# A two-layer graph attention kernel: the turn of the layers with three accumulators and chunk-wise reuse of tiles, and the prologue's weight folds on TensorE

## The chip, the cores and the metric

The kernel runs on one core of one Trainium2 chip. The metric is the device time of one launch in microseconds (us); the number given for a version is the median of its runs. A profile is of one further execution, which has a time of its own.

## The reference

6250 nodes with 256 features each, 200,000 edges sorted by their destination, two graph attention layers (4 heads of 64, then 1 head of 256), and a residual around both. Cut to what matters:

```python
def _add_self_loops(src, dst, ea, n):
    cnt = segment_sum(ones, dst, n);  sm = segment_sum(ea, dst, n)
    loop = sm / maximum(cnt, 1.0)[:, None]
    return concat([src, arange(n)]), concat([dst, arange(n)]), concat([ea, loop])

def _gat(x, src, dst, ea, Wg, a_s, a_d, Wge, a_e, b, n, h, f):
    hx = (x @ Wg).reshape(n, h, f)
    he = (ea @ Wge).reshape(-1, h, f)
    al = leaky_relu(einsum('nhf,hf->nh', hx, a_s)[src] + einsum('nhf,hf->nh', hx, a_d)[dst]
                    + einsum('ehf,hf->eh', he, a_e), 0.2)
    al = exp(al - segment_max(al, dst, n)[dst])
    al = al / segment_sum(al, dst, n)[dst]
    return segment_sum(hx[src] * al[:, :, None], dst, n).reshape(n, h * f) + b

h0 = maximum(layernorm(x), 0)
te = relu(edge_attr @ We0 + be0) * exp(h0 @ Wo0 + bo0)[src][:, None]
h1 = relu(_gat(h0, *_add_self_loops(src, dst, te, n), Wg0, as0, ad0, Wge0, ae0, bg0, 4 heads) + h0)
te = relu(edge_attr @ We1 + be1) * exp(h1 @ Wo1 + bo1)[src][:, None]
h2 = _gat(h1, *_add_self_loops(src, dst, te, n), Wg1, as1, ad1, Wge1, ae1, bg1, 1 head) + h1
return x + h2 + h0
```

All arithmetic is float32.

## The kernel before

**Tables and gathers.** For each layer a table in DRAM holds one row per node: the features times `Wg`, the node's two attention terms, and its edge factor `exp(x @ Wo + bo)`. Layer 0's table (`T[0]`, 268 numbers a row) is written in the prologue, layer 1's (`T[1]`, 260 numbers) step by step as layer 0's nodes are finished. The edges of a layer are cut into 66 steps: 64 of 24 chunks with 128 edges each, and two shorter ones at the end, 132 steps in all, numbered through both layers (step 66 is layer 1's first). For every chunk POOL issues one indirect DMA (L905) that gathers the rows of the chunk's 128 source nodes into one chunk (270 words a partition) of a tile `G`. Step k's `G` comes from the pool `gp[k % 3]`; step 0 uses a tile of its own, `G0`, whose rows are computed in the prologue instead of gathered from the table. POOL works in order: a gather that waits holds all gathers behind it.

**A step.** With the rows there, a step computes edge logits, segment maxima by scans, weights `kw`, scaled rows, and then `sums` (L1285): for each chunk two matmuls with a one-hot matrix `S` that `onehots` (L1095, 3.3 us of DVE) makes from the destination numbers. The sums of a step are merged into its nodes, and, one step later, `rows1`, `rows2` and `rows3` finish them; in layer 0 the finished row (`t1row`, one of two buffers in turn) is stored by SP into `T[1]` (L1419) and into a node table `nd` (L1421, L1424).

**The prologue.** 49 tiles of 128 nodes in nine groups of 2, 5, 7, 7, 7, 7, 7, 5 and 2 are loaded from `x` (L225, SP), and each passes through statistics (`stats`: `BN_STATS` and `BN_AGGR` on DVE, then a chain of small operations for the inverse root, on POOL for the groups from the fourth on), `norm` (ACT, L319), `turn` (PE transposes, L325, and an ACT copy, L327), `mult` (PE, L439) and `keep` (DVE, L443); a group's rows are stored into `T[0]` by SP (L344). Behind them come 24 tiles of gathered `x` rows (L255), in groups of 6 and 18, which end in `G0`. The loop over `k` (tiles) fixes the order on every engine: in each turn `step` issues the next operation of some group's statistics, and small pieces of other work (`index`, the edges' index tables; `rows0`, the gathers of `x` rows) are put in between. Before the tiles, `fold` and `fold_e` multiply the attention vectors into the weights: `Wg` times `as` and `ad` summed over a head's features give extra columns of the weight tile. They do so on DVE (L181, L183, L192, L194), from rows that a broadcast DMA spreads over all partitions; layer 1's folds run later, in the first steps (`soon`, `late`). POOL clears four node tiles `tw` (L264). `idle` gives PE nine large matmuls ahead of the first tile.

**The turn of the layers** (`ending`; a, b, c are steps 63, 64, 65, and `after` is step 66). Step 66 gathers from `T[1]` before the last rows of it are stored: its `gather` goes early into step a's tile `G`, chunk by chunk. The rows that were still lacking are read again later (`lack_rows`, L1073) and put in place by `complete` (L1083, L1084): for each of the 24 chunks two matmuls of the lacking rows with two one-hot matrices, and one DVE operation that adds the result to the kept rows. The one-hots are made by `select` (L1066, two operations of DVE) from a list of source rows, `row`. The list and the second one-hot lie in a tile of the pool `gp[2]`, the pool that step 68's gathers take their tile from next; the first one-hot lies in a tile of the one-hots' own pool. `complete` is a generator that `ending` draws from in three parts, between `parts`, `blocks`, `edge_rows` and the others of step 66. PE writes chunk c of it into accumulator c mod 3: two halves of one PSUM tile `y`, and a tile `fin`.

Of the kernel before, what the change touches and what calls it, by code (L numbers as in the profile page):

```python
# [22 lines left out]
F32 = mybir.dt.float32  # L23
# [8 lines left out]
P = 128  # L32
# [47 lines left out]
class Kernel:  # L80
# [32 lines left out]
    def consts(self, wp):  # L113
# [4 lines left out]
        self.wg, row, wpk = [], [], []  # L118
        pool = (wp, cp)
        self.ones = cp.tile([P, 1], F32, name="ones")  # L120
        nc.gpsimd.memset(self.ones, 1.0)
        self.bias, self.webd, self.be, wge = [], [], [], []
        def weights(L):

            q = (nc.scalar, nc.sync)[L.l]
            wg = cp.tile([P, 2, L.MW], F32, name=f"wg{L.l}")
            q.dma_start(wg, a[f"wg{L.l}"].rearrange("(k p) m -> p k m", p=P))
            r = pool[L.l].tile([P, 3, D], F32, name=f"row{L.l}", bufs=1)
            q.dma_start(r.rearrange("p k d -> p (k d)"), a[f"row{L.l}"][0:3 * D].partition_broadcast(P))
# [3 lines left out]
            row.append(r)  # L133
            b = cp.tile([P, L.MW], F32, name=f"bias{L.l}")
            nc.sync.dma_start(b, a[f"row{L.l}"][3 * D:].partition_broadcast(P))
            w = cp.tile([P, P + 1], F32, name=f"webd{L.l}")
            nc.sync.dma_start(w, a[f"we{L.l}"][:, 0:P + 1])
            e = pool[L.l].tile([P, D], F32, name=f"wge{L.l}", bufs=1)
            nc.sync.dma_start(e, a[f"we{L.l}"][:, P + 1:])
# [3 lines left out]
            wge.append(e)  # L143
# [31 lines left out]
        def fold(L):  # L175

            H = L.H
            for k in range(2):
                for j, c0 in ((0, L.p), (1, L.ad)):
                    t = pool[L.l].tile([P, D], F32, name=f"wtmp{L.l}", bufs=2)  # L180
                    V.tensor_mul(t, self.wg[L.l][:, k, 0:D], row[L.l][:, j, :])  # L181
                    yield
                    V.tensor_reduce(self.wg[L.l][:, k, c0:c0 + H], t.rearrange("p (h f) -> p h f", h=H),  # L183
                                    axis=AX.X, op=OP.add)
                    yield

        def fold_e(L):

            H = L.H
            wea, we1 = self.wea[L.l]  # L190
            t = pool[L.l].tile([P, D], F32, name=f"wtmp{L.l}", bufs=2)
            V.tensor_mul(t, wge[L.l], row[L.l][:, 2, :])  # L192
            yield
            V.tensor_reduce(we1, t.rearrange("p (h f) -> p h f", h=H), axis=AX.X, op=OP.add)  # L194
            yield
# [5 lines left out]
        self.late, self.soon = fold_e(self.L[1]), fold(self.L[1])  # L201
# [1444 lines left out]
```

## Time and profile before

| | us |
|---|---|
| runs | 4047.03, 4033.51, 4033.07 |
| median | 4033.51 |
| the profiled execution, its time | 4041.07 |
| its span (first to last instruction) | 4039.3 |
| POOL busy | 2998.3 (74%) |
| PE busy | 2658.8 (66%) |
| DVE busy | 2454.5 (61%) |
| ACT busy | 1117.3 (28%) |
| the first gather from a table starts at | 88.43 |
| the last one starts at | 4010.02 |

A row of the timeline reads: start, duration, engine, line, operation, the tile written and the tiles read, the count, and in brackets how long the engine was idle before and what ended that. In a row of a group the total, the mean of one in ns, and the idle time before them stand behind the count. A row of the windows holds the window, its length, and the busy time and count for PE, PE's weight load, DVE, ACT and POOL, then the granted clock, the DMA share and GB/s. Line numbers are those of the code above; in the changed kernel the same code stands some 15 to 40 lines further down.

### The profile page before, as it was taken

To read this page: it belongs to the slowest core of one execution; us is meant where nothing else is said; L and a number is where in the kernel's file an instruction comes from. 1 tells how busy PE (TensorE), PEld (TensorE's weight loads), DVE (VectorE), ACT (ScalarE), POOL (GpSimd) and SP (SyncE) were. 2 spreads that over 40 slices of the span, in tenths; PEclk is the share of its full clock that TensorE was granted. 3 is DMA by queue.
4 is the path that set the end of the run, shared out by engine and by line. 5 is a ranking of instruction groups with operands and counts; after the bars stand their busy time and mean duration, and the time that the engine had idled before them with its cause. 6 is when DMAs were issued, how large, how long until landed. Compare 5 with 4: busy or idle time off the path is not lost.

```text
span 4039.3 us, 37506 instructions
## 1 busy us (share of the span) xinstructions
PE 2658.8 (66%) x9974; PEld 1744.1 (43%) x9974; DVE 2454.5 (61%) x6096; ACT 1117.3 (28%) x2670; POOL 2998.3 (74%) x3253
## 2 busy tenths in 40 slices
PE   8776676776666676666667656656566566566565
PEld 6444444444444444444444434434334334334343
DVE  7897877877877877877864333344343343343445
ACT  5211111111111111111115434334344344343341
POOL 5777777777777777777757777777777777777775
PEclk9888888888888888888887777777777777777777
DMA  7455555555555555555545455445445445445443
GB/s 245 134 159 145 148 155 147 146 157 143 148 157 146 149 154 144 151 155 142 152 128 151 132 141 142 134 140 140 136 138 143 133 138 144 132 138 143 133 138 97
DMA packets 239747, 585.27 MB, mean 145 GB/s; under 512 B 64315, under 2 KB 96737, under 8 KB 239307
## 3 DMA queue, kind: packets, MB, share of 16 engines
q0 software_dynamic: 150144, 422.75, 39.2%
q1 hardware_dynamic: 88973, 159.40, 12.5%
q8 instruction: 85, 1.39, 0.1%
q14 instruction: 129, 1.06, 0.1%
q10 hardware_dynamic: 416, 0.67, 0.1%
HBM read 544.82 MB, written 38.12 MB: 144 GB/s over the span
## 4 chain that ended last, share of the span: by engine, by line
POOL 32%; DVE 26%; issue 14%; PE 10%; ACT 10%; DMA 8%; DVEq 0%; SPq 0%; ACTq 0%; POOLq 0%
POOL G L905 32%; ACT G L1275 8%; DVE G L1266 7%; DMA G<-T,src 7%; PE y L1005 4%; DVE S L1095 3%; PE u L1285 3%; DVE lb L1029 2%; PE ps L439 1%; DVE m L1214 1%; DVE rt L1144 1%; ACT R L1006 1%; DVE al L1162 1%; DVE al L1160 1%; DVE fb L1175 1%
## 5 line engine op out<-in xcount | busy, mean ns | idle before, releaser
L905 POOL DMA_INDIRECT G<-T,src x3102 | 2946.4, 950 | 989.9 <-issue 912.4
L1285 PE MATMUL u<-G,S 128*128 128x270 f32 (+1 forms) x6252 | 1582.8, 416 | 202.3 <-DVE G L1256 199.0
L1285 PEld LDWEIGHTS u<-G,S 128*128 128x128 f32 x6252 | 1287.4, 207 | 497.0 <-DVE G L1256 225.5
L1275 ACT ACTIVATE G<-G,kw 128x256 f32<-128x256 f32 x1512 | 609.0, 496 | 0.0
L1006 ACT ACTIVATE R<-y,webd 128x1024 f32<-128x1024 f32 (+2 forms) x264 | 235.3, 891 | 1292.9 <-PE y L1005 829.8
L1182 PE MATMUL lf<-ident,fb 128*36 128x128 f32 (+1 forms) x132 | 49.8, 377 | 765.6 <-DVE fb L1175 763.7
L1158 DVE TENSOR_TENSOR G<-rt,G 128x96 f32<-128x96 f32 (+1 forms) x132 | 30.3, 230 | 816.2 <-DMA G<-T,src 815.7
L1266 DVE TENSOR_TENSOR G<-G,kps 128x6144 f32<-128x6144 f32 (+3 forms) x77 | 440.9, 5735 | 0.0
L1095 DVE TENSOR_TENSOR S<-kps,loc 128x3072 f32<-128x3072 f32 x132 | 437.6, 3315 | 4.6
L1005 PE MATMUL y<-ea,webd 64*128 64x256 f32 (+1 forms) x1056 | 386.6, 826 | 49.9 <-ACT R L1006 49.9
L1014 PE MATMUL zad<-R,wea 128*64 128x384 f32 (+1 forms) x1056 | 295.2, 699 | 158.2 <-ACT R L1006 158.2
L1182 PEld LDWEIGHTS lf<-ident,fb 128*36 128x36 f32 (+1 forms) x132 | 15.7, 119 | 806.8 <-DVE fb L1175 804.3
L1014 PEld LDWEIGHTS zad<-R,wea 128*64 128x64 f32 x1056 | 85.2, 182 | 414.3 <-ACT R L1006 334.7
L1290 ACT ACTIVATE U<-u 128x270 f32<-128x270 f32 (+1 forms) x132 | 51.8, 392 | 642.4 <-PE u L1285 642.4
L1317 DVE SCALAR_TENSOR_TENSOR mg<-U,mw 128x1 f32<-128x1 f32 x66 | 14.5, 220 | 281.3 <-ACT mw L1315 281.3
L1005 PEld LDWEIGHTS y<-ea,webd 64*128 64x128 f32 x1056 | 122.7, 284 | 122.7 <-ACT R L1006 68.4
L1248 DVE SCALAR_TENSOR_TENSOR G<-U,kw,G 1x257 f32<-1x257 f32 x62 | 29.6, 478 | 182.6 <-ACT G L1275 182.6
L1116 PE MATMUL zad<-a,Q 128*128 128x12 bf16 (+1 forms) x132 | 26.0, 197 | 157.9 <-DVE a L1111 157.5
L439 PE MATMUL fin<-wg,h1T 128*128 128x260 f32 x264 | 126.5, 629 | 4.3 <-ACT h1T L1380 4.3
L1144 DVE STREAM_TRANSPOSE rt<-zad 128x768 f32<-128x768 f32 (+1 forms) x130 | 126.1, 970 | 4.5 <-PE zad L1130 4.5
L1029 DVE TENSOR_TENSOR lb<-lb,kps 128x1536 bf16<-128x1536 bf16 (+1 forms) x68 | 112.9, 1661 | 0.0
L1390 ACT ACTIVATE t1row<-t1row 128x1 f32<-128x1 f32 x66 | 13.4, 203 | 354.0 <-DVE t1row L443 354.0
(213 smaller groups left out, 2312.1 us busy)
## 6 DMA issues: line engine op xcount, KB each, us to landing
G<-T,src POOLq DMA_INDIRECT x3102, 2.8
ea<-in_ea_dram SPq DMA_DIRECT2D x64, 768.0 KB
lb<-locrow SPq DMA_DIRECT2D x64, 384.0 KB
nd<-t1row SPq DMA_DIRECT2D x66, 225.8 KB
tw<-nd SPq DMA_DIRECT2D x66, 225.8 KB
tw<-T SPq DMA_DIRECT2D x66, 117.2 KB
T<-t1row SPq DMA_DIRECT2D x66, 113.8 KB
tw<-in_x_dram SPq DMA_DIRECT2D x66, 112.0 KB
```

Of the source, the lines that this page charges most:

```text
L439: self.nc.tensor.matmul(ps[:, :L.MW], hT[:, k, :], self.wg[L.l][:, k, :], start=(k == 0), stop=(k == 1))
L905: nc.gpsimd.indirect_dma_start(out=G[:, c, 0:L.TW], out_offset=None, in_=self.T[L.l][0:self.N, :], in_offset=bass.IndirectOffsetOnAxis(ap= ...
L1005: nc.tensor.matmul(y[:, i, :n], self.webd[l][r, :], ea[r, w], start=True, stop=True)
L1006: nc.scalar.activation(R[:, :, w], y[:, :, :n], AF.Relu, bias=self.be[l])
L1014: nc.tensor.matmul(st["zad"][i * PH:(i + 1) * PH, o], self.wea[l][0], R[:, i, w], start=True, stop=False)
L1029: V.tensor_tensor(lb[:, :, :n], lb[:, :, :n], self.k_part.unsqueeze(2).to_broadcast([P, i, n]), op=OP.is_equal)
L1095: nc.vector.tensor_tensor(st["S"][:, c0:c1, :], self.k_iota.unsqueeze(1).to_broadcast(w), self.loc[:, o + c0:o + c1].unsqueeze(2).to_broad ...
L1144: V.transpose(rv[:, :32 * c].rearrange("p (b n) -> p b n", b=2), z.rearrange("p (b n) -> p b n", b=2)[:, :, :16 * c])
L1182: self.nc.tensor.transpose(self.lf[0:e.shape[1], 1:P + 1], e, self.ident)
L1266: nc.vector.tensor_tensor(v, v, pw[:, c0:c1, :].unsqueeze(3) .to_broadcast([P, c1 - c0, H, L.F]), op=OP.mult)
L1275: self.nc.scalar.activation(v, v, AF.Copy, scale=st["w"][:, c:c + 1])
L1285: nc.tensor.matmul(st["u"][:, :L.W], S[:, i, :], G[:, i, 0:L.W], start=(j == 0), stop=(j == c - 1))
```

## The change

In the turn of the layers: `t1row` has three buffers in place of two. `select` makes one one-hot at a call: the first is made ahead of `rows3(c)`, the second at the old place. `complete` accumulates in three tiles (`y`, `fin` and `u`, which is the tile of the sums), its first eight chunks stand ahead of `parts`, and step 66's `onehots` leave this stretch for the ordinary place in the loop. Three tiles are reused chunk by chunk, each gather waiting for what its own chunk held, where a new tile of the pool waited for the whole: `G0` for step 3, the tile of list and second one-hot for step 68, and step 66's own `G` for step 69.

In the prologue: the attention vectors come as a block matrix `att`, and `fold` and `fold_e` are done by PE (two transposes of each 128 rows of the weights, an ACT copy, two small matmuls) at the start and at tiles 12, 24 and 30, for both layers. Six `x` buffers are loaded ahead in place of four. `idle` gives three matmuls in place of nine. The node tiles are cleared by two DMAs in place of POOL's memset. The index work starts later (tile 17 in place of 11). The statistics of the first six gathered rows run between the node tiles from tile 16 on, with their chain on POOL; those of the other 18 from tile 49 on. The first edge loads (`lb`, `ea`, `fl`) are issued behind the prologue's last store.

```diff
-            self.gather(after, a["G"])
+            after["own"] = self.steps[after["k"] + 3]["own"] = a["G"]
+            self.gather(after)
...
         self.rows2(c)
+        if early:
+            self.select(after, 0)
         self.rows3(c)
...
                 self.lack_rows(after)
-                self.select(after)
+                self.select(after, 1)
                 fill = self.complete(after)
...
             self.spread(after)
+            for _ in range(C // 3):
+                next(fill, None)
             self.parts(after)
             self.blocks(after)
-            for _ in range(C // 3):
-                next(fill, None)
...
             self.edge_rows(after)
-            self.onehots(after)
             drain(fill)
+            if not early:
+                self.onehots(after)
...
+        if len(steps) > 3 and steps[3]["L"].l == 0:
+            steps[3]["own"] = self.G0
...
-        X = self.gp[2].tile([P, C, 270], F32, name="G").rearrange("p c d -> p (c d)")
+        G = self.steps[st["k"] + 2]["own"] = self.gp[2].tile([P, C, 270], F32, name="G")
+        X = G.rearrange("p c d -> p (c d)")
...
-        y = self.ps_y.tile([P, 2, 512], F32, name="y")
-        ps = (y[:, 0, :], y[:, 1, :], self.ps_f.tile([P, 512], F32, name="fin"))
+        ps = (self.ps_y.tile([P, 2, 512], F32, name="y")[:, 0, :], self.ps_f.tile([P, 512], F32, name="fin"),
+              self.ps_1.tile([P, 512], F32, name="u"))
...
-        st["trow"] = trow = self.trow1[st["s"] % 2]
+        st["trow"] = trow = self.trow1[st["s"] % 3]
...
+        def sides(w, pt):
+
+            pT = pt.tile([P, 2, P], F32, name="pT")
+            for j in range(2):
+                nc.tensor.transpose(pT[:, j, :], w[:, j * P:(j + 1) * P], self.ident)
+            t = wp.tile([P, 2, P], F32, name="hT", bufs=3)
+            nc.scalar.activation(t, pT, AF.Copy)
+            return t
+
+        def fold(L, pt):
+
+            H, at, wg = L.H, atts[L.l], self.wg[L.l]
+            ps = pt.tile([P, 512], F32, name="ps", bufs=5)
+            ts = [sides(wg[:, i, 0:D], pt) for i in range(2)]
+            for i, t in enumerate(ts):
+                for j in range(2):
+                    nc.tensor.matmul(ps[:, 2 * H * i:2 * H * i + 2 * H], t[:, j, :], at[:, j, 0:2 * H],
+                                     start=(j == 0), stop=(j == 1))
+            yield
...
-            idle(9)
+            idle(3)
+            folds = [fold(L, pt)]
+            next(folds[0])
...
-            for t in self.tws:
-                nc.gpsimd.memset(t, 0.0)
...
-                e = nc.gpsimd if 3 <= g < g0 else V
+                e = nc.gpsimd if 3 <= g <= g0 else V
...
-                    if q > (g if k >= NT - 4 else min(g, g0)):
-                        return
+                    if q > g if q < g0 else k < (16 if q == g0 else NT):
+                        continue
...
-                if k > 10 and k % 2 or k > NT:
+                if k > 16 and k % 2 or k > NT:
                     next(index, None)
...
+                if k == 8:
+                    none = a["x"][N:N + 2 * P, :].rearrange("n d -> (n d)")
+                    for i, e in ((0, 1), (M + 1, P)):
+                        w = self.tw4[i:e].rearrange("p i w -> p (i w)")
+                        n, m = w.shape
+                        nc.sync.dma_start(w, none[0:n * m].rearrange("(p w) -> p w", w=m))
+                if k in (12, 24, 30):
+                    folds.append(fold(self.L[1], pt) if k == 24 else fold_e(self.L[k // 30], pt))
+                    next(folds[0])
+                if k in (14, 26, 32):
+                    drain(folds.pop())
...
-                    self.load_lb(0)
-                    self.load_ea(0)
-                    self.load_fl(0)
...
                     store(kept)
                     kept += 1
+                    if kept == g0:
+                        self.load_lb(0)
+                        self.load_ea(0)
+                        self.load_fl(0)
```

How this moves instructions is shown at three places.

DVE at the turn of the layers, from the last node row of step 65 on, before. `t1row1` is the finished row of step 65, `S_12310` and the second half of `G_12308` are the two one-hots, `G_11781` is step 66's tile:

```order
L1370 TENSOR_TENSOR t1row1_175<-tw4_176,hw_12384 128x256
L1372 TENSOR_TENSOR t1row1_175<-t1row1_175,fb_12395 128x256
L443 TENSOR_TENSOR t1row1_175<-fin_12408,bias1_374 128x260
L1066 TENSOR_TENSOR S_12310<-G_12308,kps_116 128x3072
L1066 TENSOR_TENSOR G_12308<-G_12308,kps_116 128x3072
L1029 TENSOR_TENSOR lb_11982<-lb_11982,kps_116 128x1536
L1030 TENSOR_TENSOR Q_12426<-kps_116,qsel_570 128x256
L1108 CAST a3_12429<-tw4_176 128x1
L1109 TENSOR_TENSOR a3r_12430<-tw4_176,a3_12429 128x1
L1110 CAST a3_12429<-a3r_12430 128x1
L1111 TENSOR_TENSOR a3_12429<-a3r_12430,a3_12429 128x1
L1123 TENSOR_TENSOR aq0_170<-zad_12435,quad_122 128x4x3
```

The same place after; `G_11799` is step 66's tile, and L1121 is the operation that puts a corrected chunk in place (L1084 before):

```order
L1407 TENSOR_TENSOR t1row2_191<-tw4_192,hw_12402 128x256
L1409 TENSOR_TENSOR t1row2_191<-t1row2_191,fb_12413 128x256
L1102 TENSOR_TENSOR S_12328<-G_12326,kps_112 128x3072
L474 TENSOR_TENSOR t1row2_191<-fin_12426,bias1_370 128x260
L1102 TENSOR_TENSOR G_12326<-G_12326,kps_112 128x3072
L1065 TENSOR_TENSOR lb_12000<-lb_12000,kps_112 128x1536
L1066 TENSOR_TENSOR Q_12444<-kps_112,qsel_685 128x256
L1121 SCALAR_TENSOR_TENSOR G_11799<-G_11799,known_2408,y_12447 128x260
L1121 SCALAR_TENSOR_TENSOR G_11799<-G_11799,known_2408,fin_12448 128x260
L1121 SCALAR_TENSOR_TENSOR G_11799<-G_11799,known_2408,u_12449 128x260
```

The first one-hot has moved ahead of the row's last part, the row lies in another buffer, and the first corrections stand ahead of the small operations of `parts`.

PE in the same stretch, before: the first four chunks of `complete`, two matmuls each, behind the matmul of `parts`:

```order
L1116 MATMUL zad<-a_12429,Q 128x3
L1083 MATMUL y<-U,S 128x260
L1083 MATMUL y<-U,G 128x260
L1083 MATMUL y<-U,S 128x260
L1083 MATMUL y<-U,G 128x260
L1083 MATMUL fin<-U,S 128x260
L1083 MATMUL fin<-U,G 128x260
L1083 MATMUL y<-U,S 128x260
L1083 MATMUL y<-U,G 128x260
```

After, the last two chunks of the first eight and what follows them:

```order
L1120 MATMUL y<-U,S 128x260
L1120 MATMUL y<-U,G 128x260
L1120 MATMUL fin<-U,S 128x260
L1120 MATMUL fin<-U,G 128x260
L1153 LDWEIGHTS Q
L1153 MATMUL zad<-a_12474,Q 128x3
L1050 MATMUL zad<-R,wea_132 64x384 x4
L1167 LDWEIGHTS aq_185
L1167 MATMUL zad<-lb,aq_185 128x384
L1167 LDWEIGHTS aq_185
L1167 MATMUL zad<-lb,aq_185 128x384
L1120 MATMUL u<-U,S 128x260
```

Each chunk now has its own accumulator tile in turn, and eight of them stand ahead of `parts`.

DVE at the end of the prologue, before, from the last node tile's row (`trow_182`) on; `st_1165` takes the statistics of the 18 later gathered tiles, `mv_1166` and `sc_1167` go on with them, and the rows of `G` are the first gathered tiles' results:

```order
L443 TENSOR_TENSOR trow_182<-ps,bias_106 128x266
L274 BN_STATS st_1165<-G 128x6 x2
L619 TENSOR_SCALAR loc<-gt 128x96
L274 BN_STATS st_1165<-G 128x6 x2
L443 TENSOR_TENSOR G<-ps,bias_106 128x266
L277 BN_AGGR mv_1166<-st_1165 128x2 x8
L625 TENSOR_TENSOR gt<-gf,before 128x96
L277 BN_AGGR mv_1166<-st_1165 128x2 x8
L443 TENSOR_TENSOR G<-ps,bias_106 128x266
L277 BN_AGGR mv_1166<-st_1165 128x2 x2
L282 TENSOR_SCALAR sc_1167<-mv_1166 128x18
```

The same place after (`trow_198`, `st_1234`, `mv_1235`, `sc_1236`):

```order
L474 TENSOR_TENSOR trow_198<-ps,bias_104 128x266
L291 BN_STATS st_1234<-G 128x6 x4
L572 CAST before<-dpv 128x66
L474 TENSOR_TENSOR G<-ps,bias_104 128x266
L291 BN_STATS st_1234<-G 128x6 x4
L643 CAST gf<-gi 128x192
L474 TENSOR_TENSOR G<-ps,bias_104 128x266
L291 BN_STATS st_1234<-G 128x6 x4
L648 TENSOR_TENSOR gt<-gf,base 128x96
L291 BN_STATS st_1234<-G 128x6 x6
L294 BN_AGGR mv_1235<-st_1234 128x2 x18
L299 TENSOR_SCALAR sc_1236<-mv_1235 128x18
```

All 18 statistics now stand behind the last node tile's row, where four stood before.

More of the change, by code (lines that the diff above doesn't have):

```diff
@@ L199, in fold_e @@
             yield
-        self.late, self.soon = fold_e(self.L[1]), fold(self.L[1])
-        return fold(self.L[0]), fold_e(self.L[0]), lambda: weights(self.L[1])
+        return fold, fold_e, edge_weights, lambda: weights(self.L[1])
     def prologue(self):
@@ L229, in prologue @@
             nc.sync.dma_start(src0, a["src"][:, 0:CX])
-            for g in range(1, 3):
+            load(1)
+            fold, fold_e, edge_weights, more = self.consts(wp)
+            for g in range(2, 6):
                 load(g)
-            first, later, more = self.consts(wp)
+            edge_weights(L)
             warm = pt.tile([P, 512], F32, name="ps", bufs=5)
@@ L391, in prologue @@
                     next(rows0, None)
-                if k >= NT + 2:
-                    next(later, None)
                 if k == max(NT - 6, 7):
@@ L672, in edges @@
         self.onehots(steps[0])
-        drain(self.soon)
         self.edge_rows(steps[0])
@@ L894, in flag, with gather @@
         nc.vector.tensor_scalar(self.flag_i, f[:, 0:1], 0.0, None, op0=OP.is_equal)
-    def gather(self, st, G=None):
+    def gather(self, st):
         nc, L = self.nc, st["L"]
-        own = G is not None
+        own, G = "own" in st, st.get("own")
         if not own:
```

97 lines of the change are left out of this document (46 added, 51 removed).

## The prediction

> **What bounds the kernel now.** I read the page's groups of instructions first, with the idle time ahead of each, then the list of waits, then POOL's timeline around every long wait.
>
> ```profile
> span 4039.3 us, 37506 instructions
> L905 POOL DMA_INDIRECT G<-T,src x3102 | 2946.4, 950 | 989.9 <-issue 912.4
> POOL G L905 <- issue: 912.4, 2993, 1.0
> 88.43 0.94 POOL L905 DMA_INDIRECT G<-T,src  x1 [13.86 <-DMA tw<-in_x_dram]
> 154.53 0.94 POOL L905 DMA_INDIRECT G<-T,src  x1 [6.13 <-ACT pen L996]
> 185.08 0.94 POOL L905 DMA_INDIRECT G<-T,src  x1 [0.30 <-issue]
> 2069.10 0.94 POOL L905 DMA_INDIRECT G<-T,src  x1 [9.31 <-DMA T<-t1row]
> 2115.06 0.94 POOL L905 DMA_INDIRECT G<-T,src  x1 [16.25 <-PE fin L1083]
> 4010.02 0.95 POOL L905 DMA_INDIRECT G<-T,src  x1 [0.30 <-issue]
> ```
>
> POOL is the pacemaker. It issues 3102 gathers of 0.95 us, each with 0.30 us behind it that waits for nothing the profile shows (912.4 us over 2993 of them): 1.25 us a gather, 30.0 us for a step's 24. The first starts at 88.43, the last at 4010.02, 97% of the span. Three starts break the pace by more than the usual 0.30: step 3's first gather by 5.83, step 67's by 9.01 (the first that needs every row of layer 1's table) and step 68's by 15.95. PE, DVE and ACT run ahead of POOL otherwise, until a buffer is missing. So the time is the start of the gathers, 3102 paces, three stalls, and a tail of 28.3 us (4010.97 to 4039.3). The change leaves pace and tail; it touches the start and the stalls.
>
> **The turn of the layers.** Step 68's gathers go into the tile that holds the list of source rows and the second one-hot of `complete`. Before, the first of them waits until all of that tile is free, that is for the last correction.
>
> ```profile
> 2064.84 0.42 DVE L1370 TENSOR_TENSOR t1row<-tw,hw 128x256 f32<-128x256 f32 x1 [3.44 <-DMA nd<-t1row]
> 2065.70 0.42 DVE L443 TENSOR_TENSOR t1row<-fin,bias 128x260 f32<-128x260 f32 x1
> 2066.04 3.35 DVE L1066 TENSOR_TENSOR S<-G,kps 128x3072 f32<-128x3072 int32 x1
> 2069.30 3.35 DVE L1066 TENSOR_TENSOR G<-G,kps 128x3072 f32<-128x3072 int32 x1
> 2066.39 0.32 SPq L1419 DMA_DIRECT2D T<-t1row  x1
> 2075.37 1.22 PE L1083 MATMUL y<-U,S 128*128 128x260 f32 x2
> PEld y L1083 <- DVE G L1084: 12.3, 9, 3.4
> 2101.16 3.36 DVE L1095 TENSOR_TENSOR S<-kps,loc 128x3072 f32<-128x3072 f32 x1
> 2114.82 0.48 DVE L1084 SCALAR_TENSOR_TENSOR G<-G,known,fin 128x260 f32<-128x260 f32 x1 [0.39 <-PE fin L1083]
> 2125.76 11.87 PE L1285 MATMUL u<-G,S 128*128 128x261 f32 x48
> 2144.83 1.42 PE L1285 MATMUL u<-G,S 128*128 128x261 f32 x5
> ```
>
> The new code waits chunk by chunk. A chunk is 270 of the tile's 6480 words; the list fills the first 3072 and is last read by the second one-hot (over at 2072.65), so step 68's first gather may start when it is due, at 2115.06 - 15.95 = 2099.11. Chunk 12, due at 2099.1 + 12 x 1.25 = 2114.1, is the first that lies wholly on one-hot columns, and those belong to corrections 1 to 3, long done by then; chunk 22, due at 2126.6, is the last that needs a correction, over at 2115.3. So the wait for the tile goes even if `complete` stays as it is. **What is late next?** `complete` took 39.9 us (2075.37 to 2115.30). Three accumulators in three tiles, no longer two in halves of one, take away PE's 12.3 us of waits for DVE's read; the next step's one-hot (3.36) leaves its middle; it starts some 3 us earlier, since one select now runs in the 3.44 us in which DVE waited for a row buffer, which a third buffer ends. It ends near 2097 to 2100. Step 66's sums began 10.5 us behind its end; with the moved one-hot 3.4 more, that is about 2114, and over by 2126. Step 69 goes into step 66's tile chunk by chunk, due at 2129.1. Step 70 waits for the whole of step 67, whose sums began 19.1 us behind step 66's: over near 2145, due at 2159. None is late, with 3 us to spare even at the first. The stall of 9.01 I leave: its last store (2066.39) comes behind DVE's op at 2065.70, ahead of which there now stands a select of 3.35 in place of the wait of 3.44. **Gain 15.95 us.**
>
> **The prologue's head.** `fold` and `fold_e` move to PE, and POOL's clearing of the tw tiles becomes two DMAs.
>
> ```profile
> 12.52 2.31 DVE L282 TENSOR_SCALAR sc<-mv 128x5 f32<-128x5 f32 x1
> 12.82 1.98 POOL L264 MEMSET tw<- 128x524 f32 x4
> L282 DVE TENSOR_SCALAR sc<-mv 128x7 f32<-128x7 f32 x5 | 0.9, 170 | 0.6 <-DVE mv L277 0.5
> L181 DVE TENSOR_TENSOR wtmp<-wg,row 128x256 f32<-128x256 f32 x4 | 1.7, 423 | 0.6 <-DMA row<-in_row_dram 0.6
> L183 DVE TENSOR_REDUCE wg<-wtmp 128x4 f32<-128x256 f32 x4 | 1.7, 420 | 0.0
> 25.10 0.60 ACT L319 ACTIVATE h<-x,ln 128x256 f32<-128x256 f32 x1 [0.93 <-DVE ln L304]
> 28.34 0.38 PE L325 MATMUL pT<-ident,h 128*128 128x128 f32 x2
> 29.45 0.38 PE L325 MATMUL pT<-ident,h 128*128 128x128 f32 x2
> 34.87 0.54 DVE L464 CAST scf<-sc 128x726 f32<-128x726 int32 x1 [3.33 <-DMA sc<-in_sdst_dram]
> 45.36 0.44 PE L325 MATMUL pT<-ident,h 128*128 128x128 f32 x2 [2.37 <-ACT h L319]
> 29.67 1.06 PE L439 MATMUL ps<-wg,hT 128*128 128x266 f32 x4
> 47.70 1.89 PE L439 MATMUL ps<-wg,hT 128*128 128x266 f32 x4
> 45.30:49.40 4.10, 4.04 (x12) 3.06 (x13) 2.04 (x7) 2.39 (x7) 3.20 (x10) 0.58 0.88 355
> 83.02 0.42 DVE L443 TENSOR_TENSOR trow<-ps,bias 128x266 f32<-128x266 f32 x1
> ```
>
> The folds hold DVE for 1.7 + 1.7 = 3.4 us ahead of the norms of the eighth node tile (25.10). One `TENSOR_SCALAR` on DVE took 2.31 us beside POOL's memset, 0.17 elsewhere: 2.1 more. What comes instead (4 transposes, ACT's copies, a PSUM read) I put at 1.7, so the eighth tile is normed near 25.1 - 3.4 - 2.1 + 1.7 = 21.3. From there PE takes 1.11 us a tile at full clock (28.34 to 29.45, 1.12 with the rounding): 41 tiles, 45.9 us, and 2.2 for the last to pass through. Before, the way from 25.10 to the last node tile's keep (83.02) took 57.9, so 9.8 were lost to stalls: DVE behind an index load (3.33), which moves six tiles later, PE behind a norm (2.37) and the slow tiles after it. In their place come three more folds on PE, in order between the tiles: eight transposes at 0.19 (half of the 0.38 above) and eight small matmuls at no more than 0.26, a fourth of a tile's 1.06, make 3.6, and three waits for ACT's copies some 0.6 each: 5.5. POOL's chains, 1.2. Last keep: 21.3 + 45.9 + 2.2 + 5.5 + 1.2 = 76.1. The ends: 71.7 if the folds fill PE's gaps, and no gain at all (83) if the old stalls stay.
>
> Two rules bear on this. The granted clock was 0.58 between 45.30 and 49.40, after an idle of 2.37 us, and a tile's four matmuls took 1.89: about 0.8 a tile more, for two tiles. The Trainium skill ("TensorE: Matmul & The Clock Gate", Part 1) says that the clock halves after an idle window of about 3.4 us and comes back after as much work; by that rule a wait of 2.4 us need not have cost anything, and the trace decides otherwise. It speaks against the change, which cuts the nine warming matmuls to three and gives PE new waits for ACT: by the rows each new slow stretch is 1.6 us, and my 5.5 has room for two.
>
> The memset row goes with the Trainium skill ("SBUF — State Buffer", Who interferes with whom), by which DVE and POOL share a port pair that one of them locks for a whole instruction. That rule too has a side against the change: the first gathered rows' chain moves from DVE to POOL, some 14 small ops of 0.2 us, at most 2.8 us of blocked DVE.
>
> **The prologue's end.** The 18 later gathered rows' statistics no longer run between the node tiles, but all behind the last one.
>
> ```profile
> L274 DVE BATCH_NORM_STATS2 st<-G 128x6 f32<-128x256 f32 x24 | 9.0, 413 | 0.0
> L277 DVE BATCH_NORM_AGGREGATE mv<-st 128x2 f32<-128x6 f32 x73 | 6.5, 153 | 0.0
> 90.03 0.60 ACT L319 ACTIVATE h<-G,ln 128x256 f32<-128x256 f32 x1 [4.17 <-DVE ln L304]
> 113.53 0.43 DVE L443 TENSOR_TENSOR G<-ps,bias 128x266 f32<-128x266 f32 x1 [0.46 <-PE ps L439]
> 140.27 13.49 PE L1285 MATMUL u<-G,S 128*128 128x270 f32 x48 [0.95 <-DVE G L1266]
> 177.88 0.40 ACT L1290 ACTIVATE U<-u 128x270 f32<-128x270 f32 x1 [5.11 <-PE u L1285]
> ```
>
> Their first norm stood 7.0 us behind the last node tile's keep (83.02 to 90.03). Now 18 x 0.375 + 18 x 0.089 + three keeps and an index step (1.2) + a chain of 14 ops at 0.18 (2.5) = 12.1 us. From the norm to the last keep of G0 it is 23.9 (113.96): G0 is ready at 76.1 + 12.1 + 23.9 = 112.1, 1.9 earlier than before. Step 0's sums start 26.3 later (140.27), at 138.4; the eight fold ops of layer 1 that leave DVE on this way (before 125) gain nothing, PE's chain is as late. Step 1's sums are over 38.0 later (178.28): 176.4.
>
> POOL's side: the first gather stood 5.4 us behind the last keep (the last store to the table, issued and landed), so it starts near 81.5, 6.9 earlier. Step 0's edge loads now stand behind that store on SP's queue; they are read once G0 is ready, 30 us later, so they cost nothing unless they take that long. Step 3's gathers used to wait for the whole of step 0's tile; now each waits for its own chunk's sums, due at 141.6, begun at 138.4, and PE's 13.49 us for 24 chunks is faster than POOL's 30. That stall of 5.83 goes. Step 4 needs the whole tile of step 1: due at 81.5 + 90.2 = 171.7, free at 176.4 with 0.3 for the release: a new stall of 5, where before none was (it started at 185.08, with the sums over at 178.28). Gain 185.1 - 176.7 = **8.4 us**. It is 12.8 at the better end of the head, 1.5 at the worse.
>
> **The sum.** 15.95 + 8.4 = 24.3 us of the profiled execution's 4041.1, which gives 4016.8. The runs' median is 4033.51, 7.6 under that execution; the stalls are the same in both, so the forecast is 4033.5 - 24.3 = **4009.2 us**.
>
> **The rivals.**
> *The prologue's gain is eaten* (new folds, late statistics; the end of G0 binds, not the first gather): 1.5 to 3, and the turn's 16: 4015 to 4016, within 0.5%. For it: the 12.1 us above, and that G0 is ready only 1.9 us earlier in my own sum. Chance 0.24.
> *The turn's stall only moves*: `complete` is held by something unseen, say the shared PSUM tile of the sums (`u`), and step 69 or 70 waits 8 us: 4017. Chance 0.08.
> *Slower*: POOL issues in order, so one chunk-wise wait holds all that follows. If step 66's sums begin late, because the one-hot that left `complete` now waits on DVE behind other steps' work, step 69 waits from 2129.1. The whole change breaks even when they begin 24 us after that, at 2153, and it is 20 us slower, 4053.5, when they begin at 2173. Against it: that is 59 us behind my 2114, and a one-hot takes 3.36. Chance 0.06, with what I have not thought of.
> *It does not do what it says*: the tile is still released as a whole. Then the start of step 68 goes from 2115.1 to the end of the shorter `complete`, about 2100 against a due time of 2099.1: a point less than forecast, 4010, so this lies inside the forecast's own range.
> *PE's clock*: PE idles some 10 us behind the last node tile where it idled for about 4, and three folds make new gaps. If the clock falls in each of four places, and two tiles in each are slow by 0.8, that is 6.4, of which my sum holds about 3: 4012 to 4013. Chance 0.05. The Trainium skill's rule named above would count only the gaps over 3.4 us, and then the forecast stands.
>
> **Chances and range.** The forecast's mechanism, both gains, has 0.57. A measurement of this kernel can tell about 0.5%, 20 us, from no change, so faster means under 4013.3, and about 0.04 of the 0.57 ends above that. Faster: 0.57 - 0.04 + 0.02, half of the clock's, 0.55. Same: 0.04 + 0.24 + 0.08 + 0.03 = 0.39. Slower: 0.06. The forecast's own range is 4004 (28.8 gained, the better end of the head) to 4016 (1.5 from the prologue); with the moved stall and a second one of 5 us, and 2 at the lower end for the waits of `complete` I have not counted, 4002 to 4022.
>
> **What would show it.** Right: POOL's idle at step 68's first gather is 0.3; the last node tile's keep is near 76, the first gather near 81.5; step 3's first gather has no long idle and step 4's has some 5; `complete` is over near 2100 less the prologue's gain. Wrong: a first gather later than 86, a stall over 9 at step 4, any long idle at steps 68 to 70, or a gap at step 67 above 10.

## The result and the profile after

The changed kernel takes 4014.95 us (median of five runs, 4013.84 to 4016.44) against 4038.14 for the kernel before (five runs): 23.2 us less, a ratio of 0.9943 with a 95% interval of 0.9931 to 0.9956. Measured once more beside another version it was 4016.79 against 4037.66, 0.9948 (0.9934 to 0.9962). The forecast was 24.3 us less, and 4009.2 as a time. It started from 4033.51, the median of the first three runs of the kernel before; that of all five is 4038.14, and these 4.6 us are most of the 5.7 by which the time lies above the forecast. In some of the later measurements TensorE stopped for microseconds in the midst of its work and the kernel before took 4888.78 or 4805.48 us; the ratios measured there compare a kernel that TensorE paces, not this one.

The changed kernel's page, its first line and the group of the gathers:

```profile
span 4013.5 us, 37615 instructions
L941 POOL DMA_INDIRECT G<-T,src x3102 | 2945.2, 949 | 961.5 <-issue 910.7
```

POOL's timeline, the first gather and then the first of steps 2, 3, 4, 67 and 68, and the last of all:

```profile
82.67 0.94 POOL L941 DMA_INDIRECT G<-T,src  x1 [6.84 <-issue]
113.35 0.95 POOL L941 DMA_INDIRECT G<-T,src  x1 [0.95 <-ACT G L355]
143.35 1.01 POOL L941 DMA_INDIRECT G<-T,src  x1 [0.30 <-PE u L1322]
174.39 0.94 POOL L941 DMA_INDIRECT G<-T,src  x1 [0.87 <-PE fin L1415]
2056.82 0.94 POOL L941 DMA_INDIRECT G<-T,src  x1 [9.06 <-DVE Q L1066]
2086.84 0.95 POOL L941 DMA_INDIRECT G<-T,src  x1 [0.30 <-issue]
3981.54 0.95 POOL L941 DMA_INDIRECT G<-T,src  x1 [0.30 <-issue]
```

The last but one row is step 68's first gather, 30.0 us behind step 67's (2056.82): its 16.25 of idle time has become the usual 0.30. Step 3's first gather no longer waits (0.30, 6.13 before), and step 4's (174.39) starts 10.7 us sooner than before (185.08). Step 67's gap stays; what ends it is named by inference, a DVE operation in this view and the store into `T[1]` in the profile before. The gathers' busy time is the same to 1.2 us. The span falls by 25.8: 10.7 up to step 4, 1.6 in the 63 steps that follow, 16.2 from step 67's first gather (1940.92 to the last one before, 1924.72 now), less 2.7 by which the tail grew (29.28 behind the last gather's start before, 31.96 now).

The prologue: the eighth node tile's norm, the last node tile's keep, the first norm and the last keep of the 18 later gathered tiles, step 0's sums, and the copy behind step 1's sums:

```profile
20.08 0.60 ACT L336 ACTIVATE h<-x,ln 128x256 f32<-128x256 f32 x1 [0.53 <-DVE ln L321]
77.16 0.43 DVE L474 TENSOR_TENSOR trow<-ps,bias 128x266 f32<-128x266 f32 x1 [0.16 <-PE ps L470]
88.66 0.60 ACT L336 ACTIVATE h<-G,ln 128x256 f32<-128x256 f32 x1 [7.47 <-DVE ln L321]
112.60 0.43 DVE L474 TENSOR_TENSOR G<-ps,bias 128x266 f32<-128x266 f32 x1 [0.46 <-PE ps L470]
138.72 11.21 PE L1322 MATMUL u<-G,S 128*128 128x270 f32 x48 [0.96 <-DVE G L1303]
174.16 0.40 ACT L1327 ACTIVATE U<-u 128x270 f32<-128x270 f32 x1 [5.12 <-PE u L1322]
```

The turn: the first matmuls of `complete`, its last correction, and step 66's sums:

```profile
2058.31 1.21 PE L1120 MATMUL y<-U,S 128*128 128x260 f32 x2 [7.89 <-DMA U<-T]
2085.71 0.48 DVE L1121 SCALAR_TENSOR_TENSOR G<-G,known,u 128x260 f32<-128x260 f32 x1 [0.39 <-PE u L1120]
2096.14 11.09 PE L1322 MATMUL u<-G,S 128*128 128x261 f32 x48
```

`complete` now takes 27.9 us (39.9 before), and is over at 2086.19, 0.65 us ahead of step 68's first gather. Of PE's 12.3 us of waits for DVE in it none is left in the list of waits.

### The profile page after: what moved, and what is told of

The parts are those of the page before. It is cut to its first block, busy times and chain, and to the rows that moved or that the text cites. A ratio compares the mean times of both kernels' runs of the same rounds, so it can differ in the third digit from the quotient of the medians.

```text
span 4013.5 us, 37615 instructions
## 1 busy us (share of the span) xinstructions
PE 2655.2 (66%) x9998; PEld 1744.1 (43%) x9998; DVE 2446.4 (61%) x6071; ACT 1119.4 (28%) x2676; POOL 2998.9 (75%) x3264
## 4 chain that ended last, share of the span: by engine, by line
POOL 32%; DVE 28%; issue 14%; PE 11%; ACT 9%; DMA 7%; DVEq 0%; SPq 0%; POOLq 0%; ACTq 0%
POOL G L941 31%; DVE G L1303 8%; ACT G L1312 7%; DMA G<-T,src 7%; PE y L1041 4%; PE u L1322 4%; DVE S L1132 4%; DVE lb L1065 2%; PE ps L470 1%; DVE m L1251 1%; ACT R L1042 1%; DVE rt L1181 1%; DVE al L1199 1%; DVE al L1197 1%; DVE fb L1212 1%
```

## The experiments

**The two halves by themselves.** The theory: each removes waits of its own ahead of POOL's gathers, so they add up. The rival: the turn's stall only moves on to step 69 or 70, or the prologue's gain is eaten by G0. The first kernel is the one before with this and the new `gather`, the reuse of the tile of list and second one-hot for step 68, and the accumulators of the change:

```diff
-            self.gather(after, a["G"])
+            after["own"] = self.steps[after["k"] + 3]["own"] = a["G"]
+            self.gather(after)
...
             self.spread(after)
+            for _ in range(C // 3):
+                next(fill, None)
             self.parts(after)
             self.blocks(after)
-            for _ in range(C // 3):
-                next(fill, None)
...
-            self.onehots(after)
             drain(fill)
+            if not early:
+                self.onehots(after)
```

> The kernel before with the turn of the layers alone: three accumulator tiles, chunk-wise reuse for steps 68 and 69, the one-hot of step 66 moved out. The third row buffer and the split of the selects stay out (the buffer does not fit beside the old prologue). My theory: the idle time before step 68's first gather falls from 16.25 to 0.3 and nothing comes up at steps 69 and 70; the time falls by 16 us, a ratio near 0.996. Step 67's gap stays near 10.2. The rival in which the stall only moves: an idle of 5 us or more before step 69 or 70, and 8 to 11 us gained.

The second is the changed kernel with all of that, the third row buffer and the split of the selects undone; `G0` is still reused by chunks for step 3. So the third row buffer and the split are in neither half.

> The changed prologue, with G0 reused chunk by chunk, and the turn of the layers as it was before (two row buffers, both selects together, two halves of one accumulator tile, whole release). My theory: the two parts add up: step 4's first gather starts near 174.4 as in the full change (185.1 before), a gain of 10 to 11 us, ratio near 0.9975; the idle before step 68 is again near 16. If the parts share a gain, it is under 8.

These gave ratios of 1.0002 (0.999 to 1.0013) for the turn and 1.0027 (1.0015 to 1.0039) for the prologue, with TensorE as the pacemaker. The group of the sums' matmuls in the turn-alone kernel:

```profile
L1288 PE MATMUL u<-G,S 128*128 128x270 f32 (+1 forms) x6252 | 1871.9, 446 | 1420.7 <-issue 1188.3 <-DVE crow L1257 96.2 <-DVE G L1259 63.1
```

Two matmuls of its PE timeline, and a gather that waits behind PE:

```profile
1025.22 0.60 PE L1288 MATMUL u<-G,S 128*128 128x270 f32 x1 [2.43 <-issue]
1028.02 0.61 PE L1288 MATMUL u<-G,S 128*128 128x270 f32 x1 [2.20 <-issue]
1070.53 0.94 POOL L907 DMA_INDIRECT G<-T,src  x1 [8.43 <-PE fin L1381]
```

PE waits 1188 us for nothing that the profile shows, in pieces of 2 us and more ahead of single matmuls; its whole idle time there was 1420.7, and 202.3 in the profile before. POOL then waits ahead of step after step (4.85, 8.43 and 4.39 us ahead of three in a row), so a stall taken away at one place is waited for at the next. What stops PE is open. The halves themselves can be read from the runs in which POOL paces:

> The turn of the layers alone once more, since on the chip of the first call TensorE stopped for about 2 us ahead of single matmuls of the sums, and set the pace of every step in place of POOL. Where POOL paces: the idle time before step 68's first gather falls from 16.25 to 0.3, none comes up at steps 69 and 70, and the time falls by 16 us, ratio near 0.996. If the stall only moves: 5 us or more of idle before step 69 or 70. Where TensorE paces: no change beyond 0.2%, as in the first call.

> The changed prologue alone, once more: where POOL paces, step 4's first gather starts near 174 to 177 (185.1 before), the idle before step 68 is near 16, and the time falls by 8 to 11 us, ratio 0.9975. If the parts overlap, it falls by less than 6.

Turn alone: 4023.99 against 4036.68, ratio 0.9966 (0.9954 to 0.9979, which is 8.5 to 18.6 us). Prologue alone: 4032.4 against 4038.1, 0.9984 (0.9974 to 0.9994, 2.4 to 10.5 us). Together that makes 0.995, which agrees with the full change. POOL's timeline in the turn alone, step 68's first gather, step 3's and step 4's, and then in the prologue alone, step 4's and step 68's:

```profile
2093.18 0.94 POOL L907 DMA_INDIRECT G<-T,src  x1 [0.30 <-issue]
149.70 0.94 POOL L907 DMA_INDIRECT G<-T,src  x1 [2.96 <-ACT pen L998]
180.27 0.95 POOL L907 DMA_INDIRECT G<-T,src  x1 [0.30 <-issue]
```

```profile
175.26 0.94 POOL L938 DMA_INDIRECT G<-T,src  x1 [1.99 <-PE fin L1411]
2100.15 0.94 POOL L938 DMA_INDIRECT G<-T,src  x1 [14.98 <-PE fin L1116]
```

In the turn alone no gather of steps 68 to 70 waits more than 0.31: nothing moves. With its old prologue, step 4 starts at 180.27, though, not at the 185.08 of the profile that the forecast went by: one and the same prologue takes 5 us more or less from one profiled execution to another. The difference is step 3's wait for the whole of `G0`, 2.66 above the usual here where the forecast had read 5.83. Step 3 starts 0.77 us behind the end of step 0's sums in both, and these were over at 148.93 here and at 153.76 in the profile before: they began 2.6 us later there and took 13.49 us in place of 11.21, with a granted clock of 0.50 in their first 4 us and 1.00 here (third number from the right):

```profile
140.27:144.27 4.00, 4.00 (x9) 3.10 (x10) 3.92 (x4) 0.00 (x0) 3.09 (x4) 0.50 0.44 122
```

```profile
137.72:141.72 4.00, 4.00 (x18) 3.34 (x19) 3.93 (x4) 0.00 (x0) 3.08 (x4) 1.00 0.52 143
```

In the prologue alone step 4 starts at 175.26, and the stall of 15 is back. So the prologue's gain is some 5 to 10 us by the profiles and 5.7 by the medians, the turn's 16.0 by the profile (3854.2 us from step 4 to the end before, 3838.2 in the turn alone) and 12.7 by the medians.

**Which edit removes the turn's stall?** Two would do: chunk-wise release, or a `complete` that is over in time. Each was taken away from the full change.

```diff
-            after["own"] = self.steps[after["k"] + 3]["own"] = a["G"]
+            after["own"] = a["G"]
...
-        G = self.steps[st["k"] + 2]["own"] = self.gp[2].tile([P, C, 270], F32, name="G")
-        X = G.rearrange("p c d -> p (c d)")
+        X = self.gp[2].tile([P, C, 270], F32, name="G").rearrange("p c d -> p (c d)")
```

> The full change, but at the turn the tiles of steps 68 and 69 are released as a whole again, as before. In the changed kernel the corrections were over at 2085.9 and step 68's first gather was due at 2086.9. If the shorter run of corrections alone removes the stall, the idle before step 68 is at most 1 us and the time is that of the full change. If the chunk-wise reuse is what removes it, there is an idle of 5 us or more there. My prediction said about 1.

The reverse: the old accumulators, order and one-hots, with chunk-wise release.

> The full change with chunk-wise reuse, but with the old run of corrections: two halves of one tile and a third, the one-hot of step 66 in its middle, two row buffers, selects together. If chunk-wise reuse alone is enough, the idle before step 68 is 0.3, and since step 66's sums begin some 57 us behind step 67's first gather and step 69 is due 60 us behind it, none comes at step 69 either. If the shorter run of corrections is needed, steps 68 or 69 show an idle of 3 us or more. I expect the first, with about 3 us to spare.

Both ran while TensorE paced (4875.91 and 4915.15, single runs) and say nothing on this. Two more kernels repeat them, each with a second edit that lies 1900 us away: whole release of G0 for step 3 too (the `own` of step 3 left out), and POOL's memset put back in place of the two DMAs.

> The full change with whole release again in all three places: steps 68 and 69 at the turn, and G0 for step 3. At the turn: if the shorter run of corrections is enough by itself, step 68's idle is at most 1.5 us (the corrections were over 1 us before it was due); if chunk-wise reuse is what removes the stall, it is over 5. In the prologue: step 3's first gather waits until step 0's sums are over, near 150 in place of 143 to 145, and step 4 follows 30 us later, near 180 in place of 174.4 and 176.8: chunk-wise G0 would be worth 4 to 6 us of the prologue's gain. If step 4's own wait binds anyhow, step 4 stays under 178.

> The full change with two things as before, which stand far apart in the profile. At the turn the old run of corrections (two halves of one tile and a third, the one-hot of step 66 inside, two row buffers, selects together), with chunk-wise reuse: I expect idles of 0.3 before steps 68 and 69, with the corrections over some 40 us behind their start; if the shorter run is needed, 3 us or more there. In the prologue POOL's clearing of the node tiles in place of the two DMAs: I expect one DVE operation beside it to take near 2 us in place of 0.2 to 0.4, and the eighth tile's norm and the first gather some 2 us later (84.7); if DVE has slack there, the first gather stays near 82.6.

Whole release (4022.83): the last correction, step 68's first gather, and step 3's and 4's first gathers:

```profile
2093.46 0.48 DVE L1118 SCALAR_TENSOR_TENSOR G<-G,known,u 128x260 f32<-128x260 f32 x1 [0.40 <-PE u L1117]
2094.88 0.95 POOL L939 DMA_INDIRECT G<-T,src  x1 [0.31 <-issue]
151.07 0.94 POOL L939 DMA_INDIRECT G<-T,src  x1 [7.80 <-ACT pen L1030]
181.63 0.94 POOL L939 DMA_INDIRECT G<-T,src  x1 [0.30 <-issue]
```

At the turn nothing is lost: the corrections are over at 2093.94, 0.94 us ahead of the gather. The shorter `complete` alone takes the stall away, by a margin of a microsecond. In the prologue step 3 waits 7.5 us above the usual, and step 4 starts at 181.63 in place of 174.39 and 176.84 in the two profiles of the full change: in the new prologue reuse of `G0` by chunks is worth 5 to 7 us. Without it the new prologue's step 4 lies between the two of the old prologue (180.27 and 185.08), although its first gather starts at 82.58 in place of 87.04 and 88.43: a good part, or all, of what the folds, the memset and the order of the statistics save at the head goes into the wait for step 0's sums. No run reuses `G0` by chunks with the old prologue, so how the gain splits between the two is open.

Old `complete`, memset (4020.23): the last correction, step 68's first gather, step 66's sums, then a DVE operation and the memset beside it, and the first gather:

```profile
2105.26 0.48 DVE L1114 SCALAR_TENSOR_TENSOR G<-G,known,fin 128x260 f32<-128x260 f32 x1 [0.39 <-PE fin L1113]
2091.79 0.95 POOL L934 DMA_INDIRECT G<-T,src  x1 [0.30 <-issue]
2116.18 11.85 PE L1315 MATMUL u<-G,S 128*128 128x261 f32 x48
12.31 2.52 DVE L321 COPY ln<-sc 128x5 f32<-128x5 f32 x1
12.82 1.98 POOL L283 MEMSET tw<- 128x524 f32 x4
84.41 0.95 POOL L934 DMA_INDIRECT G<-T,src  x1 [6.12 <-ACT hT L346]
```

The corrections are over 13.9 us behind step 68's first gather, which still starts on time; step 69 starts on time too, since PE began step 66's sums at 2116.18 and it was due at 2121.8. So in these two profiles, one of each kernel, either edit alone is worth the whole 16 us, and the other adds margin only. The memset costs about what the forecast gave it: the copy, which takes 0.31 us in the changed kernel, takes 2.52, and the first gather is 1.8 us later (84.41 against 82.60 and 82.67 in the two profiles of the changed kernel). The copy there:

```profile
12.50 0.31 DVE L319 COPY ln<-sc 128x5 f32<-128x5 f32 x1
```

**The rest of step 67's gap, and the late statistics.** Two further edits on the full change: the table stores of a, b and c ahead of all `nd` stores (`rows3` does its first half, the row and its store to the table, or its last, the `nd` stores) with both selects behind the last row, and statistics of the 18 tiles from tile 42 on.

```diff
-                    if q > g if q < g0 else k < (16 if q == g0 else NT):
+                    if q > g if q < g0 else k < (16 if q == g0 else 42):
...
-            self.rows3(a)
+            self.rows3(a, last=False)
...
-            self.rows3(b)
+            self.rows3(b, last=False)
...
+        if after:
+            self.rows3(c, last=False)
+            self.rows3(a, first=False)
+            self.rows3(b, first=False)
+            self.rows3(c, first=False)
+        else:
+            self.rows3(c)
         if early:
             self.select(after, 0)
-        self.rows3(c)
```

> The full change with two further edits. At the turn the three stores into layer 1's table are issued first and the six node-table stores behind them, and both selects behind the last row; and the 18 later gathered rows' statistics run from node tile 42 on instead of 49. My theory: the 9 us ahead of step 67 are the landing of step 66's gathers and then three rounds of SP stores of 2.1 us each, so step 67 starts 3 to 4 us sooner after the last gather of step 66 (a gap of 6.5 to 7.5 in place of 10.2); and G0 is ready 4 us or more earlier, so the small waits ahead of steps 2 and 4 (0.6 each) go. Together 4 to 5 us, 4010, ratio to before 0.9932. The rival for the first: the landing of the last store sets the gap, and it stays over 9. For the second: statistics between the node tiles hold DVE, the first gather starts later than 82.7 by as much, and nothing is gained.

> The changed kernel itself, beside the one above on the same chip. Where POOL paces, ratio 0.994 to before, as recorded; the start of step 4's gathers within 3 us of 174.4, the gap at step 67 near 10.2.

4016.25 (4013.0 to 4018.25) against 4016.79 for the changed kernel on the same chip, ratios 0.9944 (0.993 to 0.9958) and 0.9948: no difference. Step 4's first gather in the changed kernel there:

```profile
176.84 0.94 POOL L941 DMA_INDIRECT G<-T,src  x1 [1.99 <-PE fin L1415]
```

The timeline of the kernel with the two edits, step 4's and step 67's first gathers on POOL and the three table stores on SP:

```profile
172.89 0.94 POOL L947 DMA_INDIRECT G<-T,src  x1 [0.30 <-issue]
2057.91 0.94 POOL L947 DMA_INDIRECT G<-T,src  x1 [9.36 <-DMA T<-t1row]
2050.65 0.33 SPq L1463 DMA_DIRECT2D T<-t1row  x1
2052.66 0.33 SPq L1463 DMA_DIRECT2D T<-t1row  x1
2054.66 0.32 SPq L1463 DMA_DIRECT2D T<-t1row  x1
```

Its list of waits over the whole span, SP's queue for the stores into `T[1]`:

```profile
SPq L1463 <- DMA T<-t1row: 3.3, 3, 1.5
```

The first edit's theory falls. With nothing between them the stores still stand 2.0 us apart, since now they wait for one another to land (3.0 of the 3.3 us, in two waits of 1.5, lie here), and the last landing releases POOL as its rival said: a gap of 10.32, where the changed kernel had 10.20. In the kernel before SP's list shows no wait of these stores for one another; there the issue of two `nd` stores fills the time between them, and the third waits 0.3 us for the row. Its first two stores, the third being at 2066.39:

```profile
2061.82 0.33 SPq L1419 DMA_DIRECT2D T<-t1row  x1
2063.88 0.32 SPq L1419 DMA_DIRECT2D T<-t1row  x1
```

The second edit does what it should at its place: the waits ahead of steps 2 and 4 are gone, and step 4 starts at 172.89, 3.95 sooner than in the changed kernel's profile beside it. Only 2.1 of that is left at step 67 and 1.3 at the last gather, and it is too little for the times to show.

**The price of the folds.** Two kernels that leave folds out: the one before without `fold` of layer 0, and the changed one without the folds at tiles 12, 24 and 30 (POOL clears a tile that they would have filled).

> The kernel before without layer 0's fold on DVE (L181, L183): layer 0's attention terms are left out of its table. It prices the folds at the head. My step: they hold DVE for 3.4 us ahead of the eighth node tile's norm, which then starts near 21.7 in place of 25.1, and the first gather 3 us earlier, near 84 to 85.4. If another engine's chain binds there, the norm moves by less than 1.5 us.

> The changed kernel without the three later folds on TensorE (tiles 12, 24 and 30): layer 0's edge attention and layer 1's attention terms are left out. It prices them on the way to the last node tile. My step: 5.5 us, so the last node tile's keep is near 71.6 in place of 77.2 and the first gather near 77. If the folds fill gaps of PE, it moves by less than 2.5 us. If the tiles are held by DVE or POOL chains, not at all.

Both ran while TensorE paced (4808.47 and 4804.36), so only the head can be read. Without the fold on DVE the eighth tile's norm starts at 22.64, 2.5 us sooner than in the profile before (25.10) and 3.8 sooner than in the disturbed profile of the turn alone (26.47). The last keep hardly moved (82.61 against 82.94 there), as PE stood still for 4.7 us right behind. Without the later folds it is at 81.32, against 85.03 in the disturbed prologue-alone profile: 3.7 us, between the two expectations. What each fold costs in the undisturbed kernel stays open.

## Why the prediction was right, step by step

- **POOL sets the pace**: right. POOL's idle time ahead of the gathers fell by 28.4 us and the span by 25.8; the tail, behind the last gather, grew by 2.7.
- **The turn, 15.95**: right, 16.2 behind step 67, none of it back at steps 69 and 70. `complete` was forecast to end 28 to 31 us behind step 67's first gather and ended 29.4 behind it; step 66's sums were forecast some 45 behind it and came 39.3 behind. Step 66's sums began 10.0 us behind the end of `complete` (10.5 before), so the 3.4 added for the moved one-hot did not show. At the end of `complete` two errors partly cancel: it started 4.8 us sooner behind that gather (1.5 in place of 6.3) where the forecast had 3, and took 27.9 where the sum of its terms gives 24.2 (39.9 - 12.3 - 3.4). The statement that the stall would go with the old `complete` too was shown. The rival that the tile is still released as a whole was given about 1 us of loss; in the run it lost nothing, by a margin of 0.94.
- **Step 67's gap stays**: right, 10.25 and 10.23 from start to start (as idle time 9.31 and 9.06, under the 10 that would have spoken against it). Its cause was read too narrowly: it is a chain of three stores, 2.0 to 2.5 us apart, and the landing of the last, 2.7 to 3.3 us; the last row alone doesn't set it.
- **The prologue's head**: the eighth norm was forecast at 21.3 and came at 20.08; the last keep at 76.1, came at 77.16; the first gather at 81.5, came at 82.67. The memset's 2.1 was confirmed at 1.8 for the first gather. From the eighth norm to the last keep it took 57.1 us, where the sum had 54.8 and the kernel before 57.9: the 5.5 for the later folds and 1.2 for POOL's chains, 6.7 together, stand against 9.0, and the early norm hid half of that, which was luck. No run shows the 1.2 or the folds' share by itself. Part of it is one of the slow stretches that the prediction feared: at the first of the three folds PE waits 1.89 us for ACT's copy (the forecast had 0.6), and the matmuls of the second and the third tile behind it take 1.98 and 1.57 us in place of 1.07, with a granted clock of 0.68 from 30 to 35 us and 1.00 from 20 to 30:

```profile
30.07 0.61 PE L208 MATMUL ps<-att,hT 128*128 128x4 f32 x4 [1.89 <-ACT hT L183]
32.00 1.98 PE L470 MATMUL ps<-wg,hT 128*128 128x266 f32 x4
```

- **The prologue's end**: 12.1 us of statistics were 11.5 (77.16 to 88.66), G0 was ready at 113.03 (forecast 112.1), step 0's sums began at 138.72 (138.4). The copy behind step 1's sums was over at 174.56, where I had 176.4: step 0's took 11.21 us in place of 13.49. A wait ahead of step 2 for G0 (0.65, and 2.2 in the second profile) was missing in the sum, but step 4's wait covers it. The new stall of 5 us at step 4, named as a sign of being right, did not come: it was 0.57 above the usual, and 1.69 in the second profile, because the first gather and step 2 were later than forecast; in the first profile step 1's sums were earlier as well. That step 1's sums bind there is still what the view shows.
- **The prologue's 8.4**: 10.7 by the profiles, but 5.7 by the medians of the half alone (2.4 to 10.5), between the forecast and the rival's 1.5 to 3. The rival's premise held: `G0` was ready hardly sooner, or later, with the new prologue (113.03 and 114.54 in the two profiles) than with the old one (113.96, and 112.00 in the turn alone). The gain is there all the same, since step 3 no longer waits for the whole of `G0`. The profile before was one with a late step 4. Taken over the profiles with the old prologue (185.08, 180.27) and the new one with chunk-wise G0 (174.39, 176.84, 175.26), it is 7.2; with the turn's 16, that is the 23.2 of the medians. So close an agreement is partly chance, with 5 us between two profiles of one prologue and halves whose medians give 12.7 and 5.7.
- **The tail**: forecast unchanged, 2.7 longer here. The granted clock around the 20 matmuls behind the last gather was 0.76 after and 1.00 before (third number from the right), by the windows of the one and then of the other; the 20 took 5.98 us in place of 4.59, which is half of the 2.7:

```profile
3981.60:3987.60 6.00, 6.00 (x23) 4.74 (x21) 2.38 (x12) 0.30 (x1) 0.88 (x1) 0.76 0.17 44
```

```profile
4009.90:4014.50 4.60, 4.60 (x23) 3.72 (x21) 2.31 (x12) 0.30 (x1) 0.95 (x1) 1.00 0.21 60
```

Counted from the last gather's start, the tail is 29.3 us in the profile before, 29.8 in the turn alone, 30.3 in the second profile of the full change and 32.1 in the prologue alone: it goes by the execution, not by the turn.

## What to carry to other kernels

Find the queue that sets the pace, list the starts that break it, and cost a change by those alone: here three starts out of 3102 held 31 us, and in the 63 steps from step 4 to step 67 the change moved 1.6 us. Ask of each stall whether one edit is enough: here a tile released by chunks and a shorter user of it each removed the same 16 us. Ask as well whether an earlier start is used: here the first gather came 4 to 6 us sooner, and where the wait for the whole of `G0` behind it was left in, no clear part of that reached step 4. Where the start of a pipeline differs by 5 us between executions, a forecast against one profile inherits that error; a second profile of the same prologue showed it, and so would one of the kernel before have done.

## What the runs showed of the hardware

Three stores of some 114 KB into one DRAM table started 2.0 us apart when nothing stood between them and each waited 1.5 us for the one before, and 2.06 and 2.51 apart with two other stores between each. A wait of PE of 1.89 us was followed by a granted clock of 0.68 (1.00 ahead of it), one of 2.37 us by 0.58. And one and the same kernel can change its pacemaker: with TensorE stopping for 2 us and more ahead of single matmuls (mean granted clock near 0.72 in place of 0.785) the kernel before took 4888.78 us in place of 4038.1, and one chip showed both at different times.
